# A planned graph network on one core: loads re-queued, ten groups in flight, the last groups' norm on another engine

## The chip, the cores and the metric

The kernel runs on one core of a Trainium2 chip. The metric is the device time of one execution in microseconds (us). Before the change the median of three runs is 1366.85 us (1366.57 to 1367.98). The profile comes from one further execution of 1367.95 us, in which the span from the first to the last instruction is 1365.1 us. Everything is computed in float32.

## What is computed

The input x is 64 batches of 256 nodes with 128 features, and adj is one 256x256 matrix. Four layers follow one another; each adds its own result to its input and normalises over the features. Cut to what matters (weights and biases come in as inputs):

```python
# layer 0: adj powers 1..3, twice the same adj, seven weight slices
x = layernorm(x + sum_k (adj^k @ x) @ weight_1[:, :, k])
# layer 1
x = layernorm(x + adj @ (x @ weight) + bias)
# layer 2: A_norm is adj + I, scaled by degree on both sides
x = layernorm(x + (A_norm @ x) @ W.T + b)
# layer 3: five gated steps, starting from h = x
for _ in range(5):
    m = adj @ h                       # m_in and m_out are the same here
    z = sigmoid([m, m] @ w3.T + w3_b + h @ u3.T + u3_b)
    r = sigmoid([m, m] @ w4.T + w4_b + h @ u3.T + u3_b)
    hv = tanh([m, m] @ w5.T + w5_b + (r * h) @ u5.T + u5_b)
    h = (1 - z) * h + z * hv
out = layernorm(x + h)
```

## The kernel before

**Groups.** Two batches make a group (`NB = 2`), so there are 32 groups, and a group's working tile is 128 partitions by 512 floats. `Group.record` (L701) writes down the operations of one group, from the load of x to the store of the output, as entries of a plan; nothing is issued there. Each of the three first layers has one propagation by adj, the fourth has one in each of its five steps. A propagation of two batches is done by `seven` (L562): seven 128x128 block products in place of eight, with three subtractions on GpSimd before (L583, L587, L590) and copies and additions on ScalarE (L624, L633) and VectorE (L611 to L621) after. A step of layer 3 further has five 128x512 products, three gates on ScalarE (L691), four elementwise operations on VectorE (L698), and, but for the last step, a rearrangement of h by a VectorE transpose and two DMAs through DRAM (`packed`, L668).

**The norms.** Layers 0 to 2 use centred weights, so that only a sum of squares is needed: squares with a running sum on ScalarE (L505), a power on GpSimd (L510), a scaling on ScalarE (L521). Layer 3 ends with a full norm: `statistics` (L475) takes mean and variance on VectorE (L481, L485), adds epsilon (L487), negates the mean (L488), and GpSimd takes the power (L491) and multiplies mean by scale (L492); `normalise` (L536) applies both on ScalarE with four activations (L541). Then the output is stored (L811).

**The end of a group.** The state is kept transposed in layer 3. For most groups it is turned back by a VectorE transpose and DMAs through DRAM (`turned` and `brought`, L803). For groups whose first batch is at or past `B - END`, that is the last four groups with `END = 8`, the turn is made by four TensorE transposes into PSUM instead (`transposes`, L809).

**The planner.** `Plan.order` (L83) is a list scheduler that runs when the kernel is built. Every entry has an engine, a cost (how long it books the engine), a lag (how long after that its readers may start) and a rank. Again and again it takes, over all engines, the ready entry that can start first; a tie goes to the lower rank. It also hands out the buffers: an entry whose buffer kind has no free slot is put off. The sorted list becomes the instruction order of every engine, and each engine then works in that order, waiting where it must. So a booked time that is wrong makes no error in the result, only an order that waits.

**What sets the order.** The rank of a group is its number. From `G - LEVEL` on, that is the last five groups with `LEVEL = 5`, it is instead a common number plus a tenth for each group and a fiftieth for each entry already recorded (L449), so these groups advance side by side, each five entries behind the one before. `ACTIVE = 8` is the number of groups in flight: the first entry of a group waits for the last entry of the group eight before (L818), and a load of x waits for the group ten before, or, in the first ten groups from the third on, for the first entry of the group two before (L823 to L825). Buffers are 8 PSUM banks, 60 general slots (`w`) and some smaller kinds (L202).

**The start.** `pre` and `load` (L214, L218) plan the loads and the preparation of the weights, all loads on SyncE's queue (SP). The first two groups (`HEAD = 4` batches) turn x on TensorE; the others do it by VectorE and DRAM (L714 to L722). SP's queue carries every DMA of the kernel.

Of the kernel before, what the change touches and what calls it, by code (L numbers as in the profile page):

```python
# [10 lines left out]
OP = mybir.AluOpType  # L11
AX = mybir.AxisListType

P = 128
NB = 2
ACTIVE = 8
HEAD = 4
LEVEL = 5
END = 8
STEPS = 5  # L20
WARM = 14
ONES = (0, 0)
# [1 line left out]
BANKS = 8  # L24
# [132 lines left out]
def kernel(  # L157
# [39 lines left out]
    def mm(o, lhsT, rhs, start, stop, shared=False):  # L197
# [1 line left out]

    SHAPES = {"bank": [P, 512], "x": [P, 512], "w": [P, 512], "th": [P, 384], "q": [P, P], "st": [P, Q * 6], "mv": [P, Q * 2],  # L200
              "ve": [P, Q], "rs": [P, Q]}
    slots = {"bank": BANKS, "x": ACTIVE + 3, "w": 60, "th": 8, "q": 8, "dram1": 8, "dram2": 16, "st": 12, "mv": 12, "ve": 24, "rs": 12}  # L202
    plan = Plan(slots)


# [5 lines left out]
    def temp(name):  # L211
        return Val("bank", SHAPES["bank"], name)

    def pre(rank, engine, cost, run, reads=(), writes=()):  # L214
        lag = {"SP": 2300, "PE": 260, "DVE": 260, "ACT": 130, "POOL": 100}[engine]
        plan.add(engine, cost, lag, rank, run, reads, writes)

    def load(rank, name, shape, src, keep=True):  # L218
        v = constant(name, shape) if keep else Val("w", shape, name)
        pre(rank, "SP", 450, lambda: nc.sync.dma_start(v.ap, src), [], [v])  # L220
        return v

    ident = const.tile([P, P], F32, name="ident")
# [136 lines left out]


    wb, wbm = constant("wb", [P, 3, C]), constant("wbm", [P, 3])
    pre(1.3, "SP", 450, lambda: nc.sync.dma_start(wb.ap[:, 0, :], w1), [], [wb])
    for i, b in ((1, b1), (2, b2)):
        pre(1.4, "SP", 450, lambda i=i, b=b: nc.sync.dma_start(
            wb.ap[:, i, :], bass.AP(tensor=b.tensor, offset=b.offset, ap=[[0, P], [1, C]])), [wb], [wb])
    pre(0.35, "DVE", 1100, lambda: centre(wb, wbm), [wb], [wb, wbm])
    w1c, b1c, b2c = ((wb, wb.ap[:, i, :]) for i in range(3))
    raw = {name: load(1.5, f"raw_{name}", [P, src.shape[1]], src, False)
           for name, src in (("w2", w2), ("w4", w4_w), ("w3", w3_w), ("w5", w5_w), ("u3", u3_w), ("u5", u5_w))}  # L370
    both = {name: Val("w", [P, C], f"both_{name}") for name in ("w4", "w3", "w5", "w34")}
    for name in ("w4", "w3", "w5"):
# [25 lines left out]

    braw, bsum = constant("braw", [P, 6]), constant("bsum", [P, 3])

    def biases():
        for i, src in enumerate((w3_b, w4_b, w5_b, u3_b, u3_b, u5_b)):
            nc.sync.dma_start(braw.ap[:, i:i + 1], src.rearrange("(p o) -> p o", o=1))

    pre(2.5, "SP", 2200, biases, [], [braw])
    pre(0.4, "DVE", 150, lambda: nc.vector.tensor_add(bsum.ap, braw.ap[:, :3], braw.ap[:, 3:]), [braw], [bsum])
    zb, rb, hb = ((bsum, bsum.ap[:, i:i + 1]) for i in range(3))

# [24 lines left out]
    class Group:  # L433
# [31 lines left out]
            return self.add("DVE", cost or dve_cost(self.width), 260, run, reads, writes, joint)  # L465

        def act(self, run, reads, writes, cost=None, joint=False):
            return self.add("ACT", cost or act_cost(self.width), 130, run, reads, writes, joint)

        def copied(self, name, ps, kind="w"):  # L470
            t = self.val(kind, name)
            self.act(lambda: nc.scalar.copy(t.ap, ps.ap), [ps], [t])
            return t

        def statistics(self, tag, s):  # L475
            st, mv, ve, rs, nm = (self.val(k, n + tag) for k, n in (
                ("st", "st"), ("mv", "mv"), ("ve", "ve"), ("rs", "rs"), ("ve", "nm")))

            def stats():
                for q in range(self.q):  # L480
                    nc.vector.bn_stats(st.ap[:, q * 6:(q + 1) * 6], nat(s)[:, q, :])  # L481

            def aggr():
                for q in range(self.q):
                    nc.vector.bn_aggr(mv.ap[:, 2 * q:2 * q + 2], st.ap[:, q * 6:(q + 1) * 6])  # L485
                mean, var = (mv.ap.rearrange("p (q k) -> p k q", k=2)[:, k] for k in range(2))
                nc.vector.tensor_scalar(ve.ap, var, EPS, None, op0=OP.add)  # L487
                nc.vector.tensor_scalar(nm.ap, mean, -1.0, None, op0=OP.mult)  # L488

            def scales():  # L490
                nc.gpsimd.tensor_tensor(rs.ap, ve.ap, half[:, :self.q], op=OP.pow)  # L491
                nc.gpsimd.tensor_tensor(mv.ap[:, :self.q], nm.ap, rs.ap, op=OP.mult)  # L492

            self.dve(stats, [s], [st], 195 * self.q)
            self.dve(aggr, [st], [mv, ve, nm], 67 * self.q + 240)
            self.add("POOL", 1420, 100, scales, [ve, nm], [rs, mv])
            return mv, rs

        def spread_of(self, tag, s):

            y, ve, rs = self.val("w", "y" + tag), self.val("ve", "ve" + tag), self.val("rs", "rs" + tag)

            def squares():
                for q in range(self.q):
                    nc.scalar.activation(nat(y)[:, q, :], nat(s)[:, q, :], AF.Square, scale=C ** -0.5,  # L505
                                         accum_out=ve.ap[:, q:q + 1])

            def scales():
                nc.gpsimd.tensor_scalar(ve.ap, ve.ap, EPS, None, op0=OP.add)  # L509
                nc.gpsimd.tensor_tensor(rs.ap, ve.ap, half[:, :self.q], op=OP.pow)  # L510

            self.act(squares, [s], [y, ve], 400 * self.q)
            self.add("POOL", 1330, 100, scales, [ve], [ve, rs])
            return y, rs

        def normalise_centred(self, tag, s):
            y, rs = self.spread_of(tag, s)

            def run():
                for q in range(self.q):  # L520
                    nc.scalar.mul(nat(y)[:, q, :], nat(s)[:, q, :], rs.ap[:, q:q + 1])  # L521

            self.act(run, [s, rs], [y], 380 * self.q)
            return y

        def added(self, tag, ps, resid):
# [4 lines left out]
        def residual(self, tag, ps, resid, left=lambda v: v.ap, right=lambda v: v.ap):  # L531
            s = self.val("w", "s" + tag)
            self.dve(lambda: nc.vector.tensor_add(right(s), left(ps), right(resid)), [ps, resid], [s])
            return (s, *self.statistics(tag, s))

        def normalise(self, tag, s, mv, rs):  # L536
            y = self.val("w", "y" + tag)

            def run():
                for q in range(self.q):  # L540
                    nc.scalar.activation(nat(y)[:, q, :], nat(s)[:, q, :], AF.Identity, bias=mv.ap[:, q:q + 1],  # L541
                                         scale=rs.ap[:, q:q + 1])

            self.act(run, [s, mv, rs], [y], 400 * self.q)
            return y

        def propagate(self, tag, h, aTs, ins=None, blocks=False, fast=True):

            if fast and self.nb == 2:
                return self.seven(tag, h, aTs, ins or tiles, blocks)  # L550
            ps, outs = self.val("bank", "pm" + tag), by_block if blocks else None

            def run():
                o, a = (outs or plain)(ps), ins or tiles
                for b in range(self.nb):
                    for kt in range(T):
                        mm(o[b], a(h)[:, b, kt], aTs.ap[:, kt, :], kt == 0, kt == T - 1)

            self.pe(pe_cost(N, self.q), run, [h, aTs], [ps])
            return self.copied("m" + tag, ps)  # L560

        def seven(self, tag, h, aTs, ins, blocks):  # L562
# [58 lines left out]
                nc.vector.tensor_tensor(o(m, slice(1, 3)), o(ps, slice(1, 3), False), both, op=OP.add)  # L621

            started = self.pe(pe_cost(P, 1), first, [h, aTs], [ps])
            kept = self.act(lambda: nc.scalar.copy(row(u, 1), row(ps, 0)), [ps], [u], act_cost(P))  # L624
            self.add("POOL", 830, 100, ts01, [h], [ts])
            self.add("POOL", 610, 100, ts2, [h, ts], [ts])
            self.add("POOL", 590, 100, ts3, [h, ts], [tq])
# [2 lines left out]
            self.dve(post11, [ps, u], [u], 215)  # L630
            self.dve(post12, [ps, u], [w], 215)
            self.dve(post13, [ps, w], [m], 215)
            self.act(lambda: nc.scalar.copy(o(m, 0), o(ps, 0, False)), [ps], [m], act_cost(P), True)  # L633
            self.pe(pe_cost(P, 2), rest, [h, tq, sums], [ps], True)
            self.dve(post2, [ps, u], [m], 340, True)
            return m
# [63 lines left out]

        def record(self):  # L701
            x_ = self.val("x", "x")
            plan.add("SP", 450, 4500 if self.start < HEAD else 2700, self.rank(), lambda: nc.sync.dma_start(nat(x_), self.view(x)), [], [x_],
                     self.load_gate)

            near = self.start < HEAD
# [22 lines left out]
            for t in range(T):  # L729
                p = self.val("bank", f"py0{t}")  # L730
                py.append(p)

                def first(p=p, t=t):
                    for b in range(self.nb):
                        o = p.ap[:, b * 2 * C:(b + 1) * 2 * C]
                        mm(o, (tiles if near else pairs)(xT)[:, b, t], w01.ap[:, 0:2, :], b == 0, True, shared=True)
                        mm(o, tiles(qT)[:, b, t], w0s.ap[:, 2:4, :], False, True, shared=True)

                def moved(p=p, t=t):
                    nc.scalar.copy(parts(v)[:, t], four(p)[:, :, 1, :])  # L740

                self.pe(pe_cost(2 * C, 2 * self.nb), first, [xT, qT, w01, w0s], [p])
                self.act(moved, [p], [v], act_cost(self.nb * C))
            for t in range(T):

                def second(p=py[t], t=t):
# [6 lines left out]
                                          four(p)[:, :, 0, :])  # L753

                self.pe(pe_cost(self.nb * C, T), second, [v, aT], [py[t]])
                self.act(summed, [py[t]], [s0], act_cost(self.nb * C))
            y = self.normalise_centred("0", s0)


# [118 lines left out]
```

## Time and profile before

The table is taken from the profile page and from a question for the busy time of engines in stretches of the span. Busy time is the time in which an engine executed at least one instruction; PE is TensorE's matmul side, DVE VectorE, ACT ScalarE, POOL GpSimd.

| Stretch of the span, us | PE busy | DVE busy | ACT busy | POOL busy |
|---|---|---|---|---|
| 0 to 40 | 33.23 | 19.93 | 16.50 | 15.20 |
| 40 to 1340 | 1290.35 | 946.23 | 734.39 | 724.28 |
| 1340 to 1365.1 | 12.12 | 16.89 | 12.81 | 7.49 |
| whole span | 1335.69 | 983.06 | 763.70 | 746.97 |

The rest of the profile is used in the prediction. A row of a group of instructions names the engine, the operation and the tiles that it writes and reads, then how many there are, their busy time and the mean of one. A row of the timeline has start and duration in us, then the instruction; a bracket at its end has the idle time of that engine just before it and what ended that idle time. A row of the waits has who waited for whom, the total in us, how often and the longest.

### The profile page before, as it was taken

To read this page: it belongs to the slowest core of one execution; us is meant where nothing else is said; L and a number is where in the kernel's file an instruction comes from. 1 tells how busy PE (TensorE), PEld (TensorE's weight loads), DVE (VectorE), ACT (ScalarE), POOL (GpSimd) and SP (SyncE) were. 2 spreads that over 40 slices of the span, in tenths; PEclk is the share of its full clock that TensorE was granted. 3 is DMA by queue.
4 is the path that set the end of the run, shared out by engine and by line. 5 is a ranking of instruction groups with operands and counts; after the bars stand their busy time and mean duration, and the time that the engine had idled before them with its cause. 6 is when DMAs were issued, how large, how long until landed. Compare 5 with 4: busy or idle time off the path is not lost.

```text
span 1365.1 us, 21963 instructions
## 1 busy us (share of the span) xinstructions
PE 1335.7 (98%) x6517; PEld 923.9 (68%) x6517; DVE 983.1 (72%) x2335; ACT 763.7 (56%) x2406; POOL 747.0 (55%) x1089
## 2 busy tenths in 40 slices
PE   8999999999999999999999999999999999999996
PEld 7986756677676666677767666766677766755553
DVE  5466777767767877776767777776766776878777
ACT  3675555555655545565565555654656556754444
POOL 3785643464765455555774554654665446843222
PEclk9999999999999999999999999999999999999998
DMA  6222233442334334333332333232433223233232
GB/s 171 63 63 71 84 101 109 123 117 84 96 93 117 98 96 124 109 95 100 109 101 78 109 118 107 86 106 80 129 101 96 85 86 93 88 114 109 79 93 60
DMA packets 269670, 134.42 MB, mean 98 GB/s; under 512 B 176368, under 2 KB 241392, under 8 KB 269552
## 3 DMA queue, kind: packets, MB, share of 16 engines
q1 hardware_dynamic: 269552, 133.03, 33.7%
q8 instruction: 52, 0.85, 0.3%
q14 instruction: 66, 0.54, 0.1%
HBM read 67.05 MB, written 65.54 MB: 97 GB/s over the span
## 4 chain that ended last, share of the span: by engine, by line
PE 89%; DVE 5%; DMA 2%; ACT 1%; issue 1%; POOL 1%; SPq 1%; ACTq 0%; POOLq 0%; DVEq 0%
PE pr L198 28%; PE ph L198 19%; PE pmg L198 18%; PE py L198 15%; PE pm L198 6%; PE pmq L198 3%; DMA x<-in_x_dram 1%; DVE hT L698 1%; DVE d L698 1%; DVE e L698 0%; DMA w_raw<-in_L_gnn_weight_dram 0%; DVE th L672 0%; DVE rh L698 0%; DVE st L481 0%; DMA wb<-in_L_gnn_b_dram 0%
## 5 line engine op out<-in xcount | busy, mean ns | idle before, releaser
L198 PE MATMUL pr<-mg,w435u5T 128*128 128x512 f32 x640 | 323.5, 595 | 2.0 <-ACT r L691 1.4
L583 POOL TENSOR_TENSOR tsg<-h 128x256 f32<-128x256 f32 x128 | 106.9, 835 | 222.4 <-DMA h<-dh 138.6
L691 ACT ACTIVATE r<-pr,bsum 128x512 f32<-128x512 f32 x160 | 109.6, 685 | 151.3 <-PE pr L198 148.1
L698 DVE TENSOR_TENSOR rh<-r,hT 128x512 f32<-128x512 f32 x160 | 123.2, 770 | 77.4 <-ACT r L691 76.8
L691 ACT ACTIVATE z<-pr,bsum 128x512 f32<-128x512 f32 x160 | 109.7, 685 | 107.7 <-PE pr L198 104.4
L698 DVE TENSOR_TENSOR d<-hv,hT 128x512 f32<-128x512 f32 x160 | 118.1, 738 | 69.5 <-ACT hv L691 68.5
L198 PE MATMUL ph<-rh,w435u5T 128*128 128x512 f32 x320 | 163.9, 595 | 1.1 <-DVE rh L698 1.1
L198 PE MATMUL ph<-mg,w435u5T 128*128 128x512 f32 x320 | 163.3, 592 | 0.0
L198 PE MATMUL pr<-hT,w2u3T 128*128 128x512 f32 x320 | 162.7, 592 | 0.0
L198 PEld LDWEIGHTS pr<-mg,w435u5T 128*128 128x128 f32 x640 | 107.1, 191 | 56.2 <-issue 38.2
L691 ACT ACTIVATE hv<-ph,bsum 128x512 f32<-128x512 f32 x160 | 109.4, 685 | 43.3 <-PE ph L198 42.7
L521 ACT ACTIVATE y<-s,rs 128x128 f32<-128x128 f32 x384 | 122.2, 393 | 13.7 <-POOL rs L510 13.3
L505 ACT ACTIVATE y<-s 128x128 f32<-128x128 f32 x384 | 113.8, 302 | 25.5 <-DVE s L528 25.3
L198 PEld LDWEIGHTS pmg<-s_aTp,tsg 128*128 128x128 f32 x768 | 102.8, 191 | 37.2 <-issue 31.1
L698 DVE TENSOR_TENSOR hT<-hT,e 128x512 f32<-128x512 f32 x160 | 123.7, 773 | 1.4
L698 DVE TENSOR_TENSOR e<-z,d 128x512 f32<-128x512 f32 x160 | 121.4, 759 | 1.9
L198 PEld LDWEIGHTS pmg<-aTp,h 128*128 128x128 f32 x512 | 88.2, 197 | 46.6 <-issue 34.9
L621 DVE TENSOR_TENSOR mg<-pmg,usg 128x256 f32<-128x256 f32 x160 | 67.1, 419 | 62.8 <-PE pmg L198 59.5
L198 PE MATMUL pmg<-s_aTp,tsg 128*128 128x128 f32 x768 | 106.6, 275 | 1.2 <-ACT usg L624 1.0
L510 POOL TENSOR_TENSOR rs<-ve,half 128x4 f32<-128x4 f32 x96 | 101.9, 1062 | 8.0
L509 POOL TENSOR_SCALAR ve<-ve 128x4 f32<-128x4 f32 x96 | 24.5, 255 | 141.8 <-ACT y L505 141.8
L198 PEld LDWEIGHTS ph<-mg,w435u5T 128*128 128x128 f32 x320 | 58.7, 190 | 63.6 <-issue 48.5
(170 smaller groups left out, 2846.9 us busy)
## 6 DMA issues: line engine op xcount, KB each, us to landing
dh<-th SPq DMA_DIRECT2D x160, 256.0 KB, 2.0
h<-dh SPq DMA_DIRECT2D x256, 128.0 KB, 2.5
x<-in_x_dram SPq DMA_DIRECT2D x32, 256.0 KB, 3.2
hT<-dh SPq DMA_DIRECT2D x128, 64.0 KB, 2.0
out_dram<-y SPq DMA_DIRECT2D x32, 256.0 KB, 2.4
dx<-tx SPq DMA_DIRECT2D x30, 256.0 KB, 2.5
xT<-dx SPq DMA_DIRECT2D x60, 128.0 KB, 2.6
dn<-tn SPq DMA_DIRECT2D x28, 256.0 KB, 2.0
```

Source lines behind the costliest of these rows:

```text
L198: nc.tensor.matmul(o, lhsT, rhs, start=start, stop=stop, skip_group_check=shared)
L505: nc.scalar.activation(nat(y)[:, q, :], nat(s)[:, q, :], AF.Square, scale=C ** -0.5, accum_out=ve.ap[:, q:q + 1])
L509: nc.gpsimd.tensor_scalar(ve.ap, ve.ap, EPS, None, op0=OP.add)
L510: nc.gpsimd.tensor_tensor(rs.ap, ve.ap, half[:, :self.q], op=OP.pow)
L521: nc.scalar.mul(nat(y)[:, q, :], nat(s)[:, q, :], rs.ap[:, q:q + 1])
L583: nc.gpsimd.tensor_tensor(ts.ap[:, :2 * P].rearrange("p (x c) -> p x c", x=2), ins(h)[:, 1], ins(h)[:, :, 0], op=OP.subtract)
L621: nc.vector.tensor_tensor(o(m, slice(1, 3)), o(ps, slice(1, 3), False), both, op=OP.add)
L691: self.act(lambda: nc.scalar.activation(t.ap, ps.ap, func, bias=bias[1], scale=1.0), [ps, bias[0]], [t], act_cost(self.width) + 100)
L698: self.dve(lambda: nc.vector.tensor_tensor(out(t), way(a), way(b), op=op), [a, b], [t])
```

## The change

Four things are edited; `PLAIN = 0` adds a condition (`self.start < B - PLAIN`) that holds for every group, and so changes nothing.

1. Loads. A load of x gets a rank lower by 1.5. The small loads of two bias vectors into `wb` and the six 128-element bias columns into `braw` move from SP's queue to GpSimd's, with ranks 0.1 and 0.2, and no longer wait for one another (`joint`). The weight loads that stay on SP get rank 0.1 in place of 1.3 to 1.5.
2. Groups in flight. `ACTIVE` goes from 8 to 10, `w` slots from 60 to 64, `th` and `q` slots from 8 to 10. The x slots follow (`ACTIVE + 3`). PSUM banks stay at 8.
3. Booked times. ScalarE's lag goes from 130 to 190 ns for the groups' entries; its booked costs go down: squares from 400 to 295 ns for each of four, the scaling from 380 to 295, the copies of 256 elements from 378 to 269, those of 128 elements from 272 to 165, the full norm from 400 to 390 for each of four. GpSimd's booking for the full norm's power goes from 1420 to 1300.
4. The end. `LEVEL` goes from 5 to 7. `END` goes from 8 to 4, so the last two groups, not four, turn h on TensorE. For these two the norm is applied on VectorE: four `tensor_scalar` (subtract mean, multiply by scale) in place of four activations, without the negated mean (L488) and the product on GpSimd (L492).

```diff
-ACTIVE = 8
+ACTIVE = 10
 HEAD = 4
-LEVEL = 5
-END = 8
+LEVEL = 7
+PLAIN = 0
+END = 4
...
-    slots = {"bank": BANKS, "x": ACTIVE + 3, "w": 60, "th": 8, "q": 8, "dram1": 8, "dram2": 16, "st": 12, "mv": 12, "ve": 24, "rs": 12}
+    slots = {"bank": BANKS, "x": ACTIVE + 3, "w": 64, "th": 10, "q": 10, "dram1": 8, "dram2": 16, "st": 12, "mv": 12, "ve": 24, "rs": 12}
...
+    QUEUES = {"SP": (nc.sync, 450), "ACT": (nc.scalar, 450), "POOL": (nc.gpsimd, 1000)}
+
+    def fetch(rank, o, src, v, queue):
+        e, cost = QUEUES[queue]
+        pre(rank, queue, cost, lambda: e.dma_start(o, src), [], [v], lag=3000, joint=True)
...
-    pre(1.3, "SP", 450, lambda: nc.sync.dma_start(wb.ap[:, 0, :], w1), [], [wb])
+    fetch(0.1, wb.ap[:, 0, :], w1, wb, "SP")
     for i, b in ((1, b1), (2, b2)):
-        pre(1.4, "SP", 450, lambda i=i, b=b: nc.sync.dma_start(
-            wb.ap[:, i, :], bass.AP(tensor=b.tensor, offset=b.offset, ap=[[0, P], [1, C]])), [wb], [wb])
+        fetch(0.1, wb.ap[:, i, :], bass.AP(tensor=b.tensor, offset=b.offset, ap=[[0, P], [1, C]]), wb, "POOL")
...
-    raw = {name: load(1.5, f"raw_{name}", [P, src.shape[1]], src, False)
+    raw = {name: load(0.1, f"raw_{name}", [P, src.shape[1]], src, False, "SP")
...
-    def biases():
-        for i, src in enumerate((w3_b, w4_b, w5_b, u3_b, u3_b, u5_b)):
-            nc.sync.dma_start(braw.ap[:, i:i + 1], src.rearrange("(p o) -> p o", o=1))
-
-    pre(2.5, "SP", 2200, biases, [], [braw])
+    for i, src in enumerate((w3_b, w4_b, w5_b, u3_b, u3_b, u5_b)):
+        fetch(0.2, braw.ap[:, i:i + 1], src.rearrange("(p o) -> p o", o=1), braw, "POOL")
...
         def act(self, run, reads, writes, cost=None, joint=False):
-            return self.add("ACT", cost or act_cost(self.width), 130, run, reads, writes, joint)
+            return self.add("ACT", cost or act_cost(self.width), 190, run, reads, writes, joint)
...
-                nc.vector.tensor_scalar(nm.ap, mean, -1.0, None, op0=OP.mult)
+                if not near:
+                    nc.vector.tensor_scalar(nm.ap, mean, -1.0, None, op0=OP.mult)
...
-            self.act(squares, [s], [y, ve], 400 * self.q)
+            self.act(squares, [s], [y, ve], 295 * self.q)
...
-            self.act(run, [s, rs], [y], 380 * self.q)
+            self.act(run, [s, rs], [y], 295 * self.q)
...
-            self.act(run, [s, mv, rs], [y], 400 * self.q)
+            def near():
+                for q in range(self.q):
+                    nc.vector.tensor_scalar(nat(y)[:, q, :], nat(s)[:, q, :], mv.ap[:, 2 * q:2 * q + 1],
+                                            rs.ap[:, q:q + 1], op0=OP.subtract, op1=OP.mult)
+
+            if self.start >= B - END:
+                self.dve(near, [s, mv, rs], [y], 257 * self.q)
+            else:
+                self.act(run, [s, mv, rs], [y], 390 * self.q)
...
-            plan.add("SP", 450, 4500 if self.start < HEAD else 2700, self.rank(), lambda: nc.sync.dma_start(nat(x_), self.view(x)), [], [x_],
+            plan.add("SP", 450, 4500 if self.start < HEAD else 2700, self.rank() - 1.5, lambda: nc.sync.dma_start(nat(x_), self.view(x)), [], [x_],
```

## The prediction

> **What bounds the kernel now.** First the page's busy table, then the busy time in three stretches (columns: stretch, length, then busy time and count of PE, its weight loads, DVE, ACT, POOL; then granted clock, DMA share, GB/s).
>
> ```profile
> PE 1335.7 (98%) x6517; PEld 923.9 (68%) x6517; DVE 983.1 (72%) x2335; ACT 763.7 (56%) x2406; POOL 747.0 (55%) x1089
> ```
>
> ```profile
> 0.00:40.00 40.00, 33.23 (x187) 29.72 (x188) 19.93 (x65) 16.50 (x55) 15.20 (x30) 1.00 0.65 179
> 40.00:1340.00 1300.00, 1290.35 (x6294) 889.00 (x6293) 946.23 (x2204) 734.39 (x2324) 724.28 (x1049) 1.00 0.34 97
> 1340.00:1365.10 25.10, 12.12 (x40) 5.19 (x38) 16.89 (x67) 12.81 (x27) 7.49 (x10) 0.84 0.18 53
> ```
>
> TensorE is the bound, and the change takes next to nothing off it: it can only shift the 29.4 us in which PE is idle, 6.8 in the first 40 us, 9.65 in the middle, 13.0 in the last 25. So each stretch is asked for its waits. The start, PE's timeline, then SP's and POOL's:
>
> ```profile
> 25.98 0.46 PE L198 MATMUL pmq<-a2T,x 128*128 128x128 f32 x2 [2.06 <-DMA x<-in_x_dram]
> 32.39 0.49 PE L198 MATMUL pmq<-a2T,x 128*128 128x128 f32 x2 [0.65 <-DMA x<-in_x_dram]
> 34.53 0.46 PE L198 MATMUL pmq<-a2T,x 128*128 128x128 f32 x2 [1.65 <-DMA x<-in_x_dram]
> ```
>
> ```profile
> 9.82 1.38 SPq L403 DMA_DIRECT2D braw<-in_L_gnn_u_b_dram  x3
> ...
> 16.83 0.58 SPq L365 DMA_DIRECT2D wb<-in_L_gnn_b_dram  x1
> 17.46 1.78 SPq L703 DMA_DIRECT2D x<-in_x_dram  x2
> ```
>
> ```profile
> 21.61 1.47 POOL L583 TENSOR_TENSOR tsq<-x 128x256 f32<-128x256 f32 x2 [15.48 <-DMA x<-in_x_dram]
> ```
>
> The reader is to see that the third group's x is issued only at 17.46, behind the small loads, and that PE later stands 4.36 us for x. In the middle PE's waits are many and short; these are the three largest (total, times, longest):
>
> ```profile
> PE pmg L198 <- ACT usg L624: 2.1, 3, 1.0
> PE py L198 <- DVE m L621: 1.1, 3, 0.4
> PE pmg L198 <- ACT s L752: 0.9, 1, 0.9
> ```
>
> Over that whole answer, 5.6 us wait for ACT (2.1, 0.9, 0.9, 0.7, 0.4, 0.3, 0.3), 3.5 for DVE, 0.2 for POOL. The end is a chain on DVE, then the last group's norm:
>
> ```profile
> 1358.70 0.17 DVE L488 TENSOR_SCALAR nm<-mv 128x4 f32<-128x4 f32 x1
> 1358.88 1.01 POOL L491 TENSOR_TENSOR rs<-ve,half 128x4 f32<-128x4 f32 x1 [1.18 <-DVE nm L488]
> 1359.96 0.20 POOL L492 TENSOR_TENSOR mv<-nm,rs 128x4 f32<-128x4 f32 x1
> 1360.19 1.65 ACT L541 ACTIVATE y<-s,mv,rs 128x128 f32<-128x128 f32 x4 [0.81 <-POOL mv L492]
> ```
>
> **What the Trainium skill says.** "Perfetto Trace Analysis", section Identifying the Most-Contended Engine: matmul occupancy is no good measure of headroom, weight-load share is. The trace agrees in part: PE shows 98% and weight loads 68%, so 98% alone proves nothing; but the chain that ended last is PE for 89%, and PE has almost no visible wait in the middle. "DMA: Bandwidth & Descriptors", section Issuing engines are not separate DMA queues: a second issuing engine saves only sequencer time. Here that time is the point: SP spends 8.50 to 11.67 and 16.83 to 17.41 issuing the eight loads that move. "SBUF — State Buffer", section Who interferes with whom: a VectorE instruction with two SBUF inputs contends with a GpSimd one that reads SBUF. The trace agrees: `e<-z,d` takes 1.02 us at 422.89 beside a GpSimd subtraction, and 0.68 at 1337.43 with GpSimd idle.
>
> **The change part by part.** Sums are against the span, 1365.1 us; the profiled execution took 1367.95, the median is 1366.85, so I subtract from the median.
>
> *Loads.* x2 needs only the first group's transposes (end about 8.5) to be issued. With rank 0.5 and the eight loads gone from SP, it goes out near 8.5, not 17.46, and lands, by its present 4.1 us, near 12.6. The later x are chained two by two through the VectorE turn (0.7 us): x4 lands near 17 (now 25.9), x6 near 21, x7 near 25 (now 34.4). All three PE waits have margins of 8 us or more. Gain 4.2 of the 4.36, bounds 0 (PE then stands for something else) and 5. x1 now goes ahead of the 448 KB layer-0 weights: these land about 1 us later (256 KB at some 230 GB/s, from the 20 to 40 stretch's 233), which shifts `w0s` from 11.1 to 12.1; its first reader runs at 14.0. Nothing.
>
> *GpSimd's eight issues.* No row shows one. Low end: SP's 0.43 us each, 3.4 us. High end: the fixed cost of 2.0 us in the skill's DMA page (section Anatomy of one DMA — SWDGE (gpsimd) path), as an estimate 16 us. I take 1.0, the planner's booking, 8 us, so GpSimd is occupied to about 9.3. Behind them waits `dinv` (now 5.42), and behind that DVE's `rows` (8.94) and PE's `p_an` turns (9.36). At 1.0 the order allows for it, and `anT` is first used at 49.0: nothing. At 2.0, PE could stand up to 5 us at `p_an`; no gain is possible here, since nothing waits for these biases until 29.46 (`yb`). Bounds 0 and +5.
>
> *ScalarE's booked times and ten groups.* No instruction is added; only the order changes. Measured spacing supports the new figures: four `y<-s,rs` take 1.28 us with 0.39 for one, so (1.28-0.39)/3 = 0.30 apart, booked 380; a 128-element copy takes 0.27, and 165 + 190 = 0.355 covers it where 272 + 130 = 0.402 did. PE can lose only where the plan put its instruction too early; of 9.4 us, 5.6 hang on ACT. Two more groups give the planner more ready products to put in such places. I take half of the 5.6, gain 3. Bounds: gain of 8 (nearly all visible idle), or a loss of 10, priced under the slower rival.
>
> *The end, last group.* Off the chain: L488 (0.08 spacing), L492 with its hand-over (1359.89 to 1360.19, 0.3), and ACT's 1.65. On it: four `tensor_scalar` of 128x128. Nearest row: L350, same shape, 0.22 for one and 0.14 to the next start (13.32 to 13.46), so 3 x 0.14 + 0.22 = 0.64 plus 0.1 of hand-over. Gain 1.2; bounds 0.8 (0.257 booked each) and 1.4.
>
> *The end, others.* Groups 29 and 30 of 32 give up four PE transposes each, on a PE with idle time: nothing. They gain a VectorE turn of 0.65 each, and a way through DRAM (2.0 to land in DRAM, about 2 to return) that hides if they are ahead of the last group. The last but one's norm adds 0.64 to DVE. DVE is busy 10.46 of 12 us from 1340 to 1352 and nearly without gap to 1358.8, so of 1.3 + 0.64 I let half stand: loss 1.0, bounds 0 and 3. `LEVEL` 7: five entries between groups as before, so the very end looks alike; two more groups feed PE, which lacks 1.2 us in that stretch. I take 0, bounds -1.2 and +2.
>
> Sum: -4.2 - 3 - 1.2 + 1.0 = -7.4. Span 1357.7, median 1359.5 us.
>
> **Rivals.** *The start and the end pay, and the middle nearly empties of waits:* of the 9.65 idle 8 goes and the tail gains 2 to 3 more. 1366.85 - 4.2 - 8 - 3 = 1351.6. For it: six tenths of the waits are ACT's, the engine whose times are corrected. Against: the waits are scattered, 0.2 to 1.0 each, as a static order leaves them.
>
> *The head's gain is given back:* layers 0 to 2 cost GpSimd as much as PE, about 12 us a group by their rows (three propagations at 1.9 to 2.0, three powers at 1.32, two `yb` at 1.32). From 60 to 100 us GpSimd is already busy 34.4 of 40; with x early and ten groups it may fill up, and PE waits there instead for the same 4 us, while the middle stays. 1366.85 - 4.2 + 4.2 - 0.2 = 1366.7, no change. Against: before 21.6 GpSimd is all but idle, and that room is now used.
>
> *Slower, ten groups on eight banks:* a propagation holds a PSUM bank from its first product until its last addition, past GpSimd's subtractions and ACT's copies. Buffers hardly grow: `w` from 7.5 to 6.4 a group, banks from 1 to 0.8. If the planner then sets products of more groups closer behind their copies, PE, which works in order, stands more often. Price: each such stand is 0.2 to 1.0 us, some 22 cost 9.4; doubled in number, +9.4. 1366.85 - 4.2 + 9.4 = 1372. It decides once the middle loses over 4 us more than now. Against: eight groups suffice to keep PE at 99.3%, and an order for ten is not bound to use them. That the change does nothing can't be: all four parts alter the order.
>
> **How the numbers follow.** Forecast 0.52, the large gain 0.20, given back 0.14, slower 0.14. Faster or slower means by over 0.2%, 2.7 us, about what a measurement of this kernel can tell from no change: faster 0.72, same 0.14, slower 0.14. The range reaches from 1348.5 (leaving out about a tenth, the far part of the large gain) to 1370, where half of the slower case is left out; it holds the head's 0 to 5 and the issue cost's +5.
>
> **What would show it.** Right: x2 issued before 10 us; no PE wait for x after 20; PE's idle time in the middle at 5 to 8 us; four VectorE instructions of 0.64 us ahead of the last store, 1.2 us sooner after the power. Wrong: GpSimd issues of 2 us and a PE stand at `p_an`; GpSimd over 95% between 20 and 100 with PE waiting for it; middle idle over 14 us; a DVE chain of the end longer than now by over 3 us.

## The result, and the profile after

The changed kernel takes **1361.7 us** (median of 4 runs, 1360.07 to 1362.56) against 1367.16 us (4 runs, one more than stood ahead, 1366.57 to 1367.98) before: a ratio of 0.9958, 95% interval 0.9941 to 0.9975. The profiled span goes from 1365.1 to 1358.3 us. The profiled execution is the fastest of the changed kernel's four (1360.07), and its span shrinks by more than the medians do (6.8 against 5.5); the last section has a possible reason.

The busy table of the changed kernel's page, then its three stretches in the columns of the prediction:

```profile
PE 1333.4 (98%) x6509; PEld 922.7 (68%) x6509; DVE 995.3 (73%) x2343; ACT 759.1 (56%) x2398; POOL 760.6 (56%) x1095
```

```profile
0.00:40.00 40.00, 34.89 (x193) 31.07 (x194) 21.97 (x66) 16.89 (x57) 21.67 (x42) 1.00 0.67 186
40.00:1340.00 1300.00, 1295.33 (x6307) 890.16 (x6306) 960.29 (x2223) 735.96 (x2329) 732.47 (x1047) 1.00 0.34 97
1340.00:1358.40 18.40, 3.23 (x12) 1.51 (x10) 13.03 (x56) 6.20 (x14) 6.42 (x8) 0.66 0.30 86
```

Length less PE's busy time gives its idle time. It falls from 6.77 to 5.11 us in the first 40 us and from 9.65 to 4.67 in the middle; in the end (to 1358.3) it rises from 12.98 to 15.07. PE's busy time falls by 2.25 us: eight 128-wide transposes have gone (some 0.8 us by their rows). The rest fits with fewer restarts, which is an inference: a pair of 512-wide products after a short pause shows 1.12 us where others show 1.02. -1.66 - 4.98 + 2.09 - 2.25 = -6.80, the change of the span. So the middle brought the most, the start little, and the end took some back.

**The start.** The changed kernel's timeline of SP's queue (start, duration of the issues), then of VectorE:

```profile
9.36 2.45 SPq L317 DMA_DIRECT2D aTp<-aT  x4
11.85 1.20 SPq L719 DMA_DIRECT2D x<-in_x_dram  x2
...
22.26 0.43 SPq L719 DMA_DIRECT2D x<-in_x_dram  x1
```

```profile
9.30 0.39 DVE L287 TENSOR_TENSOR w0s<-w_raw,ident 128x128 f32<-128x128 f32 x1 [4.03 <-DMA w_raw<-in_L_gnn_weight_dram]
...
21.14 1.30 DVE L730 STREAM_TRANSPOSE tx<-x 128x512 f32<-128x512 f32 x2
```

x2 is issued at 11.85 (with x3), not at 17.46, and lands near 15.2: GpSimd's first work on it starts at 15.19, 6.4 us sooner. But VectorE turns it at 21.14, where before it was 21.56. VectorE waits till 9.30 for `w_raw` (7.75 before; x1 now goes ahead of these weights, and small loads from GpSimd's queue run beside them, and the runs don't part the two), and then prepares weights without a gap until the turn, which its order puts last. The next x is chained to that turn, so it leaves at 22.26 in place of 22.69, and PE still waits 1.46 us for x at 33.52; in all its waits for x fall from 4.36 to 1.46. GpSimd's timeline has the moved issues:

```profile
1.28 0.77 POOL L224 DMA_DIRECT2D wb<-in_L_gnn_bias_dram  x1 [0.35 <-issue]
2.15 0.31 POOL masks.py:199 TENSOR_SCALAR_AFFINE_SELECT ident<-ident 128x128 f32<-128x128 f32 x1
...
2.97 1.69 POOL L224 DMA_DIRECT2D braw<-in_L_gnn_w_b_dram  x3
4.66 1.58 POOL L224 DMA_DIRECT2D braw<-in_L_gnn_u_b_dram  x3
```

Eight issues of 0.53 to 0.77 us, done at 6.24. The first stands between the two instructions that build the identity (the second was at 1.00 before), so PE's warm-up waits 2.52 us in place of 1.34. That alone takes 1.2 us of the start's gain. Another 0.91 us goes to a wait that is new, for the weights `raw_u` at 11.49; two small waits shrink by 0.9 together. -2.9 + 1.2 + 0.9 - 0.9 is the -1.7 of the start.

**The middle.** PE's waits between 40 and 1335 us (total, times, longest), all that are left but 0.2 us without a releaser:

```profile
PE pmq L199 <- ACT usq L640: 1.8, 2, 1.2
PE ph L199 <- DVE rh L714: 1.0, 2, 0.5
PE pmg L199 <- ACT usg L640: 0.2, 1, 0.2
```

2.0 us wait for ACT in place of 5.6, and 1.0 for DVE in place of 3.5.

**The end.** The last product of layer 3 ends at 1341.48, before at 1351.83; the rest of the span is 16.8 us, before 13.3. Busy times in the 40 us ahead of that product and after it, first of the kernel before, then of the changed one (columns as above):

```profile
1311.83:1351.83 40.00, 39.01 (x149) 21.28 (x147) 32.01 (x80) 19.50 (x39) 10.54 (x17) 1.00 0.25 71
1351.83:1365.10 13.27, 1.28 (x8) 0.84 (x8) 6.60 (x32) 5.63 (x13) 4.27 (x6) 0.69 0.27 79
```

```profile
1301.48:1341.48 40.00, 39.22 (x133) 20.34 (x132) 36.66 (x92) 20.39 (x38) 12.23 (x15) 1.00 0.35 107
1341.48:1358.30 16.82, 1.75 (x9) 1.13 (x8) 11.58 (x54) 5.51 (x13) 5.02 (x7) 0.63 0.32 92
```

VectorE's work (third pair) grows on both sides: by 4.7 us ahead of the last product and by 5.0 after it. Its timeline, with the last group's power on GpSimd and, first, SP's last loads of a turned group:

```profile
1340.17 1.74 SPq L679 DMA_DIRECT2D hn<-dn  x4
...
1336.87 0.70 DVE L667 STREAM_TRANSPOSE tn<-hT 128x512 f32<-128x512 f32 x1
...
1347.26 0.69 DVE L541 TENSOR_TENSOR s<-hn,y 128x512 f32<-128x512 f32 x1
1347.86 1.11 DVE L554 TENSOR_SCALAR y<-s,mv,rs 128x128 f32<-128x128 f32 x4
...
1352.24 1.01 POOL L498 TENSOR_TENSOR rs<-ve,half 128x4 f32<-128x4 f32 x1
...
1353.28 1.11 DVE L554 TENSOR_SCALAR y<-s,mv,rs 128x128 f32<-128x128 f32 x4 [1.12 <-POOL rs L498]
```

The last group that VectorE turns, at 1336.87, is sent to DRAM and fetched again by loads that start at 1340.17 and land by 1343.40; it is added (`s<-hn,y`) only at 1347.26, where VectorE's order has it. So the statistics of four groups, not of two, are left over for the time after the last product, and the last-but-one's norm (1347.86) runs on VectorE ahead of the last group's work. From the power's start to the end of the last norm it is 2.15 us, before 2.96.

### The profile page after: what moved, and what is told of

Its sections match the earlier page's. It is cut to its first block, busy times and chain, and to the rows that moved or that the text cites. A ratio compares the mean times of both kernels' runs of the same rounds, so it can differ in the third digit from the quotient of the medians.

```text
span 1358.3 us, 21907 instructions
## 1 busy us (share of the span) xinstructions
PE 1333.4 (98%) x6509; PEld 922.7 (68%) x6509; DVE 995.3 (73%) x2343; ACT 759.1 (56%) x2398; POOL 760.6 (56%) x1095
## 4 chain that ended last, share of the span: by engine, by line
PE 93%; DVE 3%; DMA 1%; ACT 1%; issue 1%; POOL 0%; SPq 0%; POOLq 0%; DVEq 0%; ACTq 0%
PE pr L199 29%; PE ph L199 20%; PE pmg L199 18%; PE py L199 16%; PE pm L199 7%; PE pmq L199 3%; DMA x<-in_x_dram 1%; DMA w_raw<-in_L_gnn_weight_dram 1%; DVE d L714 0%; DVE e L714 0%; DVE rh L714 0%; DVE st L487 0%; ACT y L549 0%; DVE s L541 0%; ACT y L529 0%
## 5 line engine op out<-in xcount | busy, mean ns | idle before, releaser
L599 POOL TENSOR_TENSOR tsg<-h 128x256 f32<-128x256 f32 x128 | 110.1, 860 | 213.4 <-DMA h<-dh 147.4
L714 DVE TENSOR_TENSOR d<-hv,hT 128x512 f32<-128x512 f32 x160 | 121.0, 757 | 59.6 <-ACT hv L707 59.0
L529 ACT ACTIVATE y<-s,rs 128x128 f32<-128x128 f32 x384 | 122.2, 392 | 16.8 <-POOL rs L518 16.3
L498 POOL TENSOR_TENSOR rs<-ve,half 128x4 f32<-128x4 f32 x32 | 37.8, 1180 | 142.7 <-DVE nm L495 142.1
L518 POOL TENSOR_TENSOR rs<-ve,half 128x4 f32<-128x4 f32 x96 | 104.3, 1086 | 8.0
L780 POOL TENSOR_TENSOR yb<-y,wb 128x512 f32<-128x512 f32 x64 | 84.6, 1322 | 31.7 <-ACT y L529 31.1
```

The source lines that it names most:

```text
L599: nc.gpsimd.tensor_tensor(ts.ap[:, :2 * P].rearrange("p (x c) -> p x c", x=2), ins(h)[:, 1], ins(h)[:, :, 0], op=OP.subtract)
L714: self.dve(lambda: nc.vector.tensor_tensor(out(t), way(a), way(b), op=op), [a, b], [t])
L780: nc.gpsimd.tensor_tensor(nat(yb), nat(y), bias[1][:, None, :].to_broadcast([P, self.q, C]), op=OP.add)
```

## The experiments

Twelve more measurements were made, of eleven edited kernels and of the changed kernel again; of each, one execution was profiled. Each ratio is to the kernel before as it ran beside that kernel: its median was 1367.16 for the first comparison, 1367.49 for e1 to e4, 1367.6 for e5, e6, f1 and f2, and 1367.58 for a2, g1, g2 and h1. "Idle" is PE's, for 0 to 40 / 40 to 1340 us; the last column is the time from the last product to the end of the span.

| kernel | median us | ratio (95%) | span | idle | end |
|---|---|---|---|---|---|
| before | 1367.16 | | 1365.1 | 6.77 / 9.65 | 13.3 |
| after | 1361.7 | 0.9958 (0.9941 to 0.9975) | 1358.3 | 5.11 / 4.67 | 16.8 |
| a2, after again | 1363.06 | 0.9964 (0.995 to 0.9977) | 1360.0 | 5.45 / 4.42 | 16.8 |
| e1, LEVEL 5 | 1369.89 | 1.0017 (1.001 to 1.0024) | 1366.4 | 4.79 / 8.74 | 17.4 |
| e2, eight groups | 1370.64 | 1.0028 (1.0017 to 1.0039) | 1370.7 | 6.10 / 10.10 | 17.0 |
| g2, nine groups | 1365.44 | 0.9984 (0.9975 to 0.9992) | 1363.6 | 5.81 / 6.44 | 17.0 |
| f2, twelve groups | 1376.56 | 1.0063 (1.0048 to 1.0078) | 1375.9 | 5.60 / 12.16 | 17.0 |
| e3, old ScalarE times | 1363.39 | 0.9974 (0.9967 to 0.998) | 1360.9 | 6.33 / 5.30 | 16.7 |
| e4, old loads | 1361.39 | 0.9961 (0.9945 to 0.9976) | 1361.0 | 6.98 / 4.21 | 16.5 |
| e5, turns on TensorE | 1362.41 | 0.9962 (0.9949 to 0.9974) | 1359.7 | 5.95 / 4.23 | 14.4 |
| e6, norms on ScalarE | 1362.66 | 0.9962 (0.9947 to 0.9977) | 1360.7 | 5.96 / 4.21 | 16.7 |
| f1, gate of x | 1359.99 | 0.9944 (0.993 to 0.9959) | 1357.5 | 4.25 / 5.79 | 17.0 |
| g1, before + ten + LEVEL 7 | 1368.35 | 1.0003 (0.9995 to 1.0012) | 1366.2 | 4.23 / 9.14 | 14.1 |
| h1, three edits | 1357.61 | 0.9924 (0.9912 to 0.9937) | 1355.6 | 4.64 / 5.46 | 13.1 |

### Undoing one part at a time

**e1: the level.**

```diff
-LEVEL = 7
+LEVEL = 5
```

> The changed kernel with LEVEL back at 5. Theory A (levelling moves work into a VectorE-bound end): with five level groups VectorE has fewer groups' last steps together; PE's last 512-wide product comes later than 1341.5, by 3 to 8 us, but the stretch from it to the end of the span shrinks from 16.8 to 12 to 14 us; the time as a whole changes little, 1359 to 1364. Theory B (levelling is what keeps PE fed up to 1335): PE idle in the 135 us before the end goes from 0 to 3 or more, the end stays 16 to 17 us, 1364 to 1367.

TensorE's order is the changed kernel's until about 975 us, and then loses: 4.22 us of its 8.74 idle lie between 1100 and 1200. The end is not shorter (17.4). So theory A falls: a level of 7 isn't what lengthens the end, and without it the whole gain is gone. Of theory B the wait in the 135 us before the end doesn't come either (0.3 us); the loss lies earlier and is larger than it named.

**e2: groups in flight.**

```diff
-ACTIVE = 10
+ACTIVE = 8
```

> The changed kernel with eight groups in flight (the 64 general slots stay). Theory A (the middle was won by ScalarE's booked times): PE idle from 40 to 1340 stays at 4 to 6 us and the time at 1360 to 1363. Theory B (it was won by the two more groups): PE idle in the middle goes back to 8 to 11 us, the time to 1365 to 1368.

The number also sets the x slots (11 now, not 13) and which group a load of x waits for. The middle idles as much as before (10.10, 4.45 of it from 800 to 1000), and with the long end the kernel is slower than before, by more than theory B named. As theory B had it, with eight groups the middle's gain is gone.

**e3: ScalarE's booked times.** All entries of the diff's third part go back (GpSimd's power apart); its core:

```diff
-            return self.add("ACT", cost or act_cost(self.width), 190, run, reads, writes, joint)
+            return self.add("ACT", cost or act_cost(self.width), 130, run, reads, writes, joint)
...
-            self.act(squares, [s], [y, ve], 295 * self.q)
+            self.act(squares, [s], [y, ve], 400 * self.q)
...
-            self.act(run, [s, rs], [y], 295 * self.q)
+            self.act(run, [s, rs], [y], 380 * self.q)
```

> The changed kernel with ScalarE's old booked times and lag. Theory A (the middle was won by the booked times): PE idle from 40 to 1340 goes back to 8 to 11 us with more than half of it waiting for ScalarE, time 1365 to 1368. Theory B (by the two more groups): PE idle stays at 4 to 6, time 1360 to 1363.

PE idles 5.30 us in the middle: of the 5.0 us gained there, 4.35 stay without the corrected times. Its median is 1.7 us above the changed kernel's, 0.3 above its repeat a2 and 0.4 above theory B's range. The prediction had put the gain on this part (theory A); nearly all of it stands without it, as theory B says.

**e4: the loads.** The first part goes back as a whole; its core:

```diff
-    fetch(0.1, wb.ap[:, 0, :], w1, wb, "SP")
+    pre(1.3, "SP", 450, lambda: nc.sync.dma_start(wb.ap[:, 0, :], w1), [], [wb])
...
-            plan.add("SP", 450, 4500 if self.start < HEAD else 2700, self.rank() - 1.5, lambda: ...
+            plan.add("SP", 450, 4500 if self.start < HEAD else 2700, self.rank(), lambda: ...
```

> The changed kernel with all loads in their old order and on SP's queue. Theory A (the loads are worth what the first 40 us show, 1.7 us of PE idle): PE idle from 0 to 40 goes from 5.1 back to 6.5 to 7, PE waits for x about 4 us, time 1362.5 to 1364.5. Theory B (the early x are also what filled the middle): PE idle in the middle rises above 7 as well, 1366 or more. Theory C (nothing, GpSimd's issues and the late identity cost as much as is won): 1360.5 to 1362.

PE idles 1.9 us longer in the first 40 us and 0.46 less in the middle; the median is the same as with the new loads. From about 14 us on TensorE's order is the changed kernel's, so beside the other parts the loads add nothing to the middle's gain. The idle time is as theory A expected, the time as theory C. What the loads are worth can't be told from nothing with these runs; 4 us, the prediction's figure, would show.

**e5: the turn of the last groups, e6: their norm.** Each undoes one half of what the fourth part does by `END`. In e5 groups 29 and 30 are turned by TensorE again, in e6 the last two norms are ScalarE's.

```diff
+TURN = 8
...
-            if self.start < B - END:
+            if self.start < B - TURN:
```

> The changed kernel, but with the turn of h on TensorE for the last four groups again (the norm on VectorE stays with the last two). Theory A (the end is bound by VectorE, and the two turns of 0.65 us each that came to it lengthen it): from the last 512-wide product to the end of the span 15.5 us in place of 16.8, time 1360 to 1361. Theory B (those turns lie beside PE's last products, the end is as long without them): 16.5 to 17 us, 1361.5 to 1362.5.

```diff
-            return (s, *self.statistics(tag, s, self.start >= B - END))
+            return (s, *self.statistics(tag, s, False))
...
-            if self.start >= B - END:
+            if False:
```

> The changed kernel with the norm of the last two groups on ScalarE again (mean negated on VectorE, product on GpSimd). Theory A (the prediction: the last group gains by the move): the stretch from the last power to the end grows by 0.8 to 1.2 us, time 1362.5 to 1363. Theory B (what VectorE loses with the last but one's norm outweighs it): the stretch from the last 512-wide product to the end shrinks below 16.5, time 1361 to 1361.7.

The two start and run alike (idle 5.95 / 4.23 and 5.96 / 4.21; TensorE's order is the changed kernel's throughout in e6, until 1332 us in e5), so their ends can be set side by side. With TensorE's turns the end is 14.4 us, with ScalarE's norms 16.7, as in the changed kernel. e5's time after the last product:

```profile
1345.32:1359.70 14.38, 1.75 (x9) 1.13 (x8) 9.10 (x39) 3.13 (x8) 3.67 (x4) 0.63 0.29 87
```

VectorE has 9.10 us to do there, not 11.58. The extra turns on TensorE put the last product 1.3 us later (1345.32 against e6's 1343.98). The net is -1.0 in the span and nothing that the medians show: for e5 theory A holds for the stretch and theory B for the time. e6's last power on GpSimd and the norms of the last two groups on ScalarE:

```profile
1353.90 1.01 POOL L498 TENSOR_TENSOR rs<-ve,half 128x4 f32<-128x4 f32 x1
1353.91 3.18 ACT L549 ACTIVATE y<-s,mv,rs 128x128 f32<-128x128 f32 x8 [1.67 <-POOL mv L500]
```

From that power's start to the end of the last norm it is 3.19 us, in the changed kernel 2.15: the 1.04 us that theory A expected. But from the last product to that power it is 9.92 us, in the changed kernel 10.76, where the last-but-one's norm stands in VectorE's way. What the norm on VectorE gains for the last group, it loses ahead of it, and the end is the same within 0.1 us. The turns through DRAM make the end long.

### What stands behind the middle

**f2, g2: twelve and nine groups**, with the x slots of f2 kept at 13 (g2 has 12).

```diff
-ACTIVE = 10
+ACTIVE = 12
...
-    slots = {"bank": BANKS, "x": ACTIVE + 3, "w": 64,
+    slots = {"bank": BANKS, "x": 13, "w": 64,
```

> The changed kernel with twelve groups in flight, all slots left as they are. Theory A (more ready products go on filling the middle): PE idle from 40 to 1200 falls from 3.9 to 2 or less, time 1358 to 1360.5. Theory B (eight banks and 64 slots are used up by ten groups): no change within 1 us. Theory C (groups closer behind one another wait for one another): over 1364.

```diff
-ACTIVE = 10
+ACTIVE = 9
```

> The changed kernel with nine groups in flight, slots left. Theory A (each group more gives the planner more to fill with): between eight and ten, 1364.5 to 1367.5. Theory B (the time of one order says little of its neighbour's: single long stands decide): outside that, under 1363 or over 1369.

f2 went as theory C expected, g2 as theory A: eight, nine, ten, twelve groups give 1370.6, 1365.4, 1361.7, 1376.6 us. Twelve is slower, as a rival of the prediction had it for ten, but not in that rival's way, by twice as many small waits: PE waits 16 times from 40 to 1335 us, before 20 times. The largest single piece is one stand, and a stretch at half rate after it (the eight products at 787.81 take 1.91 us, later ones of that shape 1.06):

```profile
785.54 0.77 PE L199 MATMUL pm<-s_anT,y 128*128 128x128 f32 x2 [3.82 <-DVE m L633]
...
787.81 1.91 PE L199 MATMUL py<-w2u3T,m 128*128 128x128 f32 x8
```

**g1: the two numbers alone.** To the kernel before, only ten groups with the larger buffers, and the level; loads, booked times and end are those of before.

```diff
-ACTIVE = 8
+ACTIVE = 10
-LEVEL = 5
+LEVEL = 7
```

> The kernel before with ten groups in flight, the slots of the change and LEVEL 7, and nothing else. Theory A (these two carry the gain, the rest is small): 1361.5 to 1364, PE idle from 40 to 1340 at 4 to 6 us. Theory B (the gain is a match of all the parts, since leaving any out of the large ones cost 8 to 9 us and more than the whole gain): 1365 to 1371, PE idle in the middle over 8.

No gain (theory B): 1.0003. The middle idles 9.14 us, 4.24 of it between 600 and 800. The two largest of PE's waits in the middle:

```profile
PE pmg L198 <- DVE mg L617: 1.8, 3, 1.3
PE pmg L198 <- ACT usg L624: 1.5, 3, 0.9
```

So taking out either number loses 8 to 9 us against the changed kernel (7 to 8 against its repeat), more than the whole gain, and the two alone give nothing. Against the changed kernel the middle needs neither the new loads (e4) nor the last groups' turn and norm (e5, e6), and hardly the booked times (e3); with all of these back at once (g1) its gain is gone. No part owns it. Each bad order has a few stands of about 1 to 4 us in a place of its own (1100 to 1200, 800 to 1000, 600 to 800, 785).

The idle time is only a part of what they lose. PE's busy time, 1333.44 us in the changed kernel's profile and 1334.30 in its repeat, is 1337.19 in e1, 1338.50 in e2, 1338.29 in g1 and 1342.15 in f2. Some of it is clock: g1 has half the clock for 3.4 us from 26 us and for 6.8 us from 627 us. By half of that time, as an estimate, it lost 5 us there, so g1's order may be better than its time says. Why the planner makes the stands in these places and not elsewhere stays open: it would have to be followed through its choices, which was not done.

### The start once more

**f1: the gate of the x loads.** The later loads of x wait for the first group's first entry, not for the turn of the group two before.

```diff
-            group.load_gate = (groups[i - 2].first,)
+            group.load_gate = (groups[0].first,)
```

> The changed kernel with the loads of x of groups 4 to 11 waiting for the first group's first entry in place of the VectorE turn two groups before. Theory A (the head's gain stopped at the turn queued behind VectorE's preparation, 21.1 us): x of groups 4 to 7 lands before 24, PE's wait for x (1.46 us) goes, PE idle from 0 to 40 falls from 5.1 to 3.5, time 1359.5 to 1361. Theory B (what the start saves is given back, as with the old loads): PE idle in the first 40 us falls, time 1361 to 1362.5.

SP's timeline now has the loads in a row, and PE has no wait for x at all, as theory A expected:

```profile
12.53 2.31 SPq L719 DMA_DIRECT2D x<-in_x_dram  x4
...
17.38 3.77 SPq L719 DMA_DIRECT2D x<-in_x_dram  x6
```

That shows the chain through the VectorE turn as the cause of the wait that was left. Its worth is less sure: PE's idle time in the first 40 us falls to 4.25, not to 3.5, since the waits for weights grow by 0.8; the median is 1359.99 us against 1361.7, and the two intervals overlap.

**a2: the changed kernel again**, to see what one profile is worth.

> The changed kernel once more, unaltered, to hold the others against in the same call. All theories: 1360.5 to 1362.5. If its PE waits over 1.5 us for x in the first 40 us, theory D (a wait for x also costs clock) expects half-rate matmuls for some 3 us after it and a span longer by about 2 us than the first profile's 1358.3; if the wait is shorter, full rate.

1363.06 us, 1.4 above the first time. PE waits only 0.5 us for x, where theory D expected the full rate; half rate came all the same, after waits for weights. So theory D fails as it stood. The order is the same, yet the profiled span is 1.7 us longer; where that lies is told in the last section.

### A version that beats both

**h1** keeps the changed kernel and adds the gate of f1, turns the last four groups on TensorE as e5 does, and leaves the norm on VectorE to the very last group.

```diff
-END = 4
+END = 2
+TURN = 8
...
-            if self.start < B - END:
+            if self.start < B - TURN:
...
-            group.load_gate = (groups[i - 2].first,)
+            group.load_gate = (groups[0].first,)
```

> The changed kernel with three edits the runs point to: loads of x of groups 4 to 11 gated by the first group's first entry; turn of h on TensorE for the last four groups; the norm on VectorE for the very last group alone. Theory A (each adds up: 1.7 from the gate, about 1 from the last but one's norm leaving the VectorE chain, 0 to 1 from the turns): 1357 to 1359, last 512-wide product to the end 14 us or less. Theory B (what the end saves is given back by later last products, as with the turns alone): 1359.5 to 1361.

1357.61 us (1356.82 to 1358.58, 5 runs), ratio 0.9924, as theory A expected; no run of the changed kernel reached that. It is 5.4 us under a2, which ran beside it, more than the 2.7 to 3.7 that theory A adds up; what each edit brings in this company was not tested. After the last product:

```profile
1342.51:1355.60 13.09, 1.28 (x8) 0.84 (x8) 8.24 (x36) 4.78 (x12) 3.87 (x5) 0.72 0.32 95
```

VectorE has 8.24 us left there and the end is as short as it was before the change, while the middle (5.46 idle) keeps most of its gain.

## Why the prediction came out as it did

The forecast time (1359.5) is 2.2 us below the measured one, and the span's change, -6.8, is near the sum of -7.4. What holds is that the change wins mainly in PE's waits (4.55 of the 6.80 us of span). That the size is so near is luck, for errors cancel: the start brought 1.7 and not 4.2, the middle 5.0 and not 3, the end took 2.1 of idle time where its two terms together were to give 0.2, and PE's busy time, off which the change was to take next to nothing, fell by 2.25. None of the four signs of being right came as stated (x2 left at 11.85; PE waited for x at 33.52; the middle idled 4.67; the four instructions took 1.11 us), and one sign of being wrong came.

- *Loads, -4.2.* Mis-sized: the waits for x fell by 2.9, and the start's idle by 1.7. The step that failed is "x4 lands near 17". It took the turn as following the landing; VectorE was still busy with the weights until 21.14, so x4 was issued at 22.26, as before. Nor did x2 go out at 8.5: the transposes of the first groups began only at 9.32, and SP sent four copies of `aTp` first. f1 shows the chain as the cause; e4 shows no worth in the median.
- *"w0s shifts by 1 us: nothing."* The shift came (VectorE starts at 9.30, not 7.75), but the reader that mattered was not `w0s`'s own: it was the turn of x2, which stands behind all of this work in VectorE's order.
- *GpSimd's issues, 1.0 us each, nothing.* 0.53 to 0.77, below the value taken and within the bounds. The 1.2 us at the warm-up came from where the first issue was put, ahead of the identity's second instruction. The prediction looked only at what is queued behind the issues at `dinv`. Nor is it so that nothing waited for these biases until 29.46: in the kernel before VectorE stands 3.24 us for `wb` till 20.26, just ahead of the turn of x2.
- *Booked times and ten groups, -3.* Right in sign, too small (5.0), and its reasoning failed: half of ScalarE's waits was to go because its times were corrected. e3 leaves 4.35 of the 5.0 with the old times; e2, e1 and g1 show that the numbers of groups and level, with the rest of the order, decide.
- *Last group, -1.2.* Measured -0.9 (2.96 to 2.15 us, and 0.08 for L488). The mis-sized term is the four `tensor_scalar`: 1.11 us, not 0.64. The row taken from L350 has one operation and no operand that changes per partition; these have two of each, and which of it costs the time isn't shown. Set against e6 the move gains 1.04 us after the last power, but that power comes 0.84 us later for the last-but-one's norm, which the prediction has in the next term, at half of 0.64.
- *Other end, +1.0, bounds 0 and 3.* Mis-sized, the largest error: from the last product to the end it is 3.5 us more, and without the last group's 0.9 it would be 4.4. "A way through DRAM that hides if they are ahead of the last group" fails: at the end four groups advance side by side, the turned group lands 6.5 us after its turn began (1336.87 to 1343.40), and VectorE adds it 10.4 us after (1347.26), just ahead of the last group. The prediction's own sign of being wrong, a VectorE chain longer by over 3 us, is what the trace shows (11.58 us of work after the last product, before 6.60).
- *The rivals.* The large gain did not come: the middle kept 4.67 us of idle time, and the tail gained nothing. "Head gain given back" did not happen by GpSimd. "Slower, ten groups on eight banks" did not happen at ten; twelve is slower (1376.56), but by single stands and clock, not by a doubling of small waits.

## What to carry to other kernels

Where a static list schedule drives a kernel that is 98% busy on one engine, a parameter changes the whole order: undo each part before giving it a price, since here two numbers were each worth about 8 us in the full set and, put in without the rest, nothing. An earlier load gains only if every step behind it also moves: follow it past the landing to the engine that handles it next, and to what that engine has queued. At the end of a kernel, count the work of the engine that is last busy after the bound engine's last product, and give that work to the idle one, as h1 does. Before two profiled spans are set against each other, see whether the clock was the same in both.

## What the hardware showed unexpectedly

**After a short wait TensorE can run at half rate for 3.4 us.** In e6, PE waits 1.68 us for x and then runs pairs of products at 1.06 us that later take 0.60; the granted clock between 20 and 40 us is 0.91. PE's timeline there:

```profile
34.31 0.83 PE L199 MATMUL pmq<-a2T,x 128*128 128x128 f32 x4 [1.68 <-DMA x<-in_x_dram]
34.93 1.06 PE L199 MATMUL py<-w0p,xT 128*128 128x256 f32 x2
...
38.24 0.60 PE L199 MATMUL py<-w0p,xT 128*128 128x256 f32 x2
```

In a2 the same happens near 13 us, after waits of 0.85 and 1.39 for weights: eight products take 3.37 us there, in the first profile of the same program 1.89. That 1.5 us is most of the 1.7 between the two spans.

```profile
12.83 0.33 PE L397 MATMUL p_w2u3T<-ident,raw_u 128*128 128x128 f32 x1 [1.39 <-DMA raw_u<-in_L_gnn_u_w_dram]
13.00 3.37 PE L199 MATMUL pmq<-a2T,x 128*128 128x256 f32 x8
```

This is the common case here: in ten of the fourteen profiles the granted clock is 0.50 for 3.4 us somewhere in the first 40 us, each time after a wait of PE; only before, after, e3 and f1 keep the full clock there. So the changed kernel's first profile had the better of two cases, and profiled spans less than 1.7 us apart (half of 3.4, an estimate of what one such stretch costs) prove little. The length of the wait doesn't decide it: the kernel before waits 2.06 us at 25.98 and keeps the full clock, g1 waits 2.16 at 25.81 and loses it; e3's waits of 0.73 and 1.28 for x leave the clock full, e4's of 0.83 and 1.30 don't. In f2 the stand of 3.82 us is followed by half the clock from 784.7 to 791.6, about 6.8 us. The Trainium skill's "TensorE: Matmul & The Clock Gate", section Part 1: The HAM clock gate, says that the clock falls to half after an idle window of about 3.4 us, that it takes a busy window of that length to come back, and that the window runs freely, so that the same kernel varies. The traces agree on the half rate, on the length of the slow stretch (3.4 us, and twice that in f2 and g1) and on the variation; but waits far shorter than that window were followed by it here, 1.68 us in e6 and 1.18 in e2. What decides it is not shown.
